# Layer 1's self-attention: score banks handed out and masked in pairs

## The chip, the cores and the metric

The kernel runs on one core of a Trainium2 chip. The metric is the device time of one execution in microseconds (us). A core has five engines that run their own instruction queues side by side: TensorE (matmuls, PE in the profile; its weight loads are PEld), VectorE (DVE), ScalarE (ACT), GpSimd (POOL) and SyncE (SP). Matmuls write into PSUM, which has eight banks of 512 fp32 columns on 128 partitions; VectorE and ScalarE carry the results into SBUF.

## The reference, cut to what matters

A two-layer decoder on 32 batches of 100 tokens of width 256: in each layer self-attention, cross-attention to a context, and a mixture of experts. The change is in layer 1's self-attention, which has 16 heads of width 16 and no softmax: scores above the diagonal are set to zero and multiplied with the values as they are.

```python
kqv = x @ W1 + b1                       # x is layer-normed, (32, 100, 256)
k, q, v = jnp.split(kqv, 3, axis=-1)    # each to (32, 16 heads, 100, 16)
mask = jnp.tril(jnp.ones((t, t), dtype=bool))
attn = jnp.where(mask, jnp.einsum('bhqd,bhkd->bhqk', q, k), 0.0)
out = jnp.einsum('bhqk,bhkd->bhqd', attn, v)
...
return out @ W2 + b2                    # added to x
```

## The kernel before, in words

The stages follow each other: layer 0's three parts, then `l1_attn`, `l1_xattn` and `l1_ffn`. All arithmetic is fp32. The activations lie in SBUF as 25 tiles of 128 rows (`self.x`), so a batch of 100 rows straddles tiles.

`l1_attn` begins with work of the next stage (`ahead`: 15 value projections of the cross-attention), turns the first seven tiles of norm rows (`turn`, `norm_turn`), projects queries and keys of the first four batches (`proj`) and then loops over the batches. Step b issues on TensorE, in this order:

- S, `scores(b)`: 16 small matmuls of 32 rows by 100 columns, heads in four row groups r = 0 to 3, that go round four banks, one per row group (400 of its 512 columns are used).
- P, `proj(b0 + 4, i)`: one of four projections for the next four batches. ScalarE copies the result out (one or two copies, L973, L976).
- V, `vals(b + 1)`: the values of the next batch; two VectorE adds carry them out (L986).
- Z, `values(b - 1)`: masked scores times values, of the batch before; ScalarE copies them out (L1022).
- O, `out(b - 2)`: output projection of a tile that is complete, in 25 of the steps; one VectorE add (L261).
- Turns: in the fourth step of a group of four batches, two of `norm_turn` for tiles of a later group; in a few steps one for the cross-attention (`next_norm`, `later`). A copy on VectorE or ScalarE in turn carries them out (L151, L150).

The masks are VectorE's: in `scores`, four multiplications with `keep`, the transposed lower triangle, each from one bank of PSUM into an `s` tile of SBUF (L1005). VectorE also adds the rows that GpSimd gathers from layer 0's experts (`gather0`, L1264 and L1269, two for each tile, spread over the first three steps of a group), and computes norm statistics and norm rows (L197 to L209). In the later groups nothing is left to gather.

The order on TensorE is the program's (`manual_schedule`). On the other engines a planner sets the order at compile time, by its own costs and by what is ready; each engine then runs its queue strictly in that order, with semaphores between the engines.

PSUM is handed out by tag: `self.psum.tile(..., bufs=n)` gives one of n buffers, and the taker waits until the previous user's last reader is done. Here all helpers (`bank_s`, `bank_m`, `bank_z`, `bank_t`) take from one tag of eight banks, in TensorE's order.

Of the kernel before, what the change touches and what calls it, by code (L numbers as in the profile page):

```python
# [9 lines left out]
F32 = mybir.dt.float32  # L10
# [3 lines left out]
ALU = mybir.AluOpType  # L14
AX = mybir.AxisListType

P = 128
NB = 32
T = 100
# [80 lines left out]
class Kernel:  # L100
# [26 lines left out]
        return self.tc.tile_pool(name=f"ps{name}", bufs=1, space=bass.MemoryType.PSUM)  # L127

    def bank(self, tag):
        if tag not in self.n_banks:  # L130
            tag = "t"
        return self.psum.tile([P, 512], F32, tag=tag, name=f"ps_{tag}", bufs=self.n_banks[tag])

    def bank_s(self):
        return self.bank("s")
# [91 lines left out]
    def norm_turn(self, f, n, xn, bank):  # L227
        pt = bank[:, : NK * n * P].rearrange("p (k c) -> p k c", k=NK)
        for k in range(NK):
            for j in range(n):  # L230
                self.nc.tensor.transpose(  # L231
                    pt[:, k, j * P : (j + 1) * P], xn[:, j, k * P : (k + 1) * P], self.ident,
                )
        self.evac(self.xnT[:, :, f * P : (f + n) * P], pt)
# [687 lines left out]
    def l1_attn(self):  # L922
        nc, tc, a = self.nc, self.tc, self.a
        with ExitStack() as st:
            self.psum = st.enter_context(self.banks("l1a", t=8))
            wk, wq, wv, wo, bqk, bv, bo, xbo = self.w1a
            cp = st.enter_context(tc.tile_pool(name="c1a", bufs=1))
            pool = st.enter_context(tc.tile_pool(name="p1a", bufs=2))
            for f in range(FRONT1[0]):
                self.gather0(pool, f)  # L930
            keep = self.tri(cp, "keepT", 1, -1, 1.0, 0.0)
# [18 lines left out]
            q, k, s, later = {}, {}, {}, deque()  # L950
# [39 lines left out]
            def rows_of(r):  # L990
                return slice(32 * r, 32 * r + 32)


            def scores(b):
                cols = slice((b % 4) * T, (b % 4 + 1) * T)
                ps = [self.bank_s()[:T, : 4 * T].rearrange("p (c j t) -> p c j t", c=2, j=2) for _ in range(4)]
                for c in range(2):
                    for j in range(2):
                        for r in range(4):
                            self.mm(ps[r][:, c, j, :], [(  # L1000
                                k[b // 4][rows_of(r), c, cols], q[b // 4][rows_of(r), c, j, cols]
                            )])
                for r in range(4):
                    t = s[b, r] = pool.tile([T, 2, 2, T], F32, tag="s", name="s", bufs=8)
                    nc.vector.tensor_tensor(  # L1005
                        t.rearrange("p c j t -> p (c j) t"), ps[r].rearrange("p c j t -> p (c j) t"),
                        self.mid(keep, 4), ALU.mult,
                    )

            def values(b):  # L1010
                pz = self.bank_z()[:, : 2 * T].rearrange("p (c t) -> p c t", c=2)
                for c in range(2):
                    for j in range(2):
                        for r in range(4):
                            nc.tensor.matmul(  # L1015
                                pz[rows_of(r), c, :], lhsT=vs[b % 3][:, 8 * c + 2 * r + j, :],
                                rhs=s[b, r][:, c, j, :], start=(j == 0), stop=(j == 1),
                            )
                for r in range(4):
                    del s[b, r]  # L1020
                for z, cols in self.z_parts(b):
                    nc.scalar.copy(z, pz[:, :, cols])  # L1022
# [33 lines left out]
            with tc.manual_schedule(engines={mybir.EngineType.PE}):  # L1056
# [17 lines left out]
                for b in range(NB + 2):  # L1074
                    i = b % 4
                    b0 = b - i
                    if b < NB:
                        scores(b)
                    if b0 + 4 < NB:
                        proj(b0 + 4, i)  # L1080
                    if b + 1 < NB:
                        vals(b + 1)
                    if 0 < b <= NB:
                        values(b - 1)
                    if b > 1:
                        out(b - 2)
                    if b0 + 8 < NB:
                        fs = group(b0 // 4 + 2)
                        if i < 3:
                            self.gather0(pool, fs[i], self.last_row)  # L1090
                            self.norm_stats(fs[i], FRONT1)
                        else:
                            turn(fs[0], 2)
                            turn(fs[2], 1)
                    if later:
                        later.popleft()()
                    if waiting:
                        next_norm()
# [996 lines left out]
```

## Time and profile before

| | |
|---|---|
| median of 3 runs | 2956.52 us (2954.38 to 2960.02) |
| the profiled execution | 2956.08 us, its span 2954.3 us |
| TensorE busy | 2851.3 us, 97% of the span |
| VectorE busy | 1787.6 us, 61% |
| ScalarE busy | 1412.4 us, 48% |
| `l1_attn`'s loop over batches | about 1620 to 1793 us of the span |

The profile is of one execution. A row of the timeline gives the start and length in us, the engine, the line, the operation with its tiles (out<-in) and form, and how many instructions it merges; in brackets how long the engine's queue stood idle before and what ended that. A matmul's row is one of TensorE, with the matching weight loads in a row of PEld; fp32 matmuls appear as two instructions each. `L156` is the helper `mm`, so the tiles tell its callers apart: `ps_t<-qT,kT` are scores, `ps_t<-xnT,wB` projections, `ps_t<-wB,xnT` values' inputs, `ps_t<-s,v` (L1015) values, `ps_t<-wB,zT` output projections. The end of a matmul is modelled, so a busy TensorE may in part be waiting: a stretch of the same work that is longer than usual, with an idle bracket at its weight loads, is a wait.

### The profile page before, as it was taken

The page shows a single profiled execution, that of the slowest core. Times are in us where ns is not written, and L with a number is a line of the kernel's source. Part 1 is how long each engine was busy: PE and PEld are TensorE (multiplying, and loading weights), DVE is VectorE, ACT ScalarE, POOL GpSimd, SP SyncE. Part 2 cuts the span into 40 slices and gives each one's busy share as a digit, 9 for nine tenths or more (in the row PEclk, how much of TensorE's full clock was granted, in tenths as well). Part 3 has the DMA queues.
Part 4 walks back from the last instruction along what each step waited for, and adds up shares of the span by engine and source line. Part 5 has one row for each costly group of instructions (what it writes and reads, how often), then busy time and mean ns, then how long its engine had stood idle before and what let it go on. Part 6 is the DMA issues. An engine that isn't in the chain of part 4 may idle for free. (4 is left out here: it accounts for less than half of the span.)

```text
span 2954.3 us, 66469 instructions
## 1 busy us (share of the span) xinstructions
PE 2851.3 (97%) x26012; PEld 2172.6 (74%) x26012; DVE 1787.6 (61%) x5120; ACT 1412.4 (48%) x4261; POOL 913.0 (31%) x1040
## 2 busy tenths in 40 slices
PE   8999999999999999999998999999999999999993
PEld 7777777677777766888886667777777777776672
DVE  6666665577777762222224878676676776776553
ACT  5555555467676641222223224565666565657320
POOL 3222221266666536100003621011302213123373
PEclk9999999999999989999999999999999999999996
DMA  9880000000000004564553100010000000000396
GB/s 319 269 290 1 1 1 1 12 15 16 16 16 16 10 29 147 191 223 181 194 215 112 49 4 10 6 38 25 26 10 13 10 9 16 12 11 5 97 227 189
DMA packets 127510, 224.11 MB, mean 76 GB/s; under 512 B 39470, under 2 KB 105446, under 8 KB 120401
## 3 DMA queue, kind: packets, MB, share of 16 engines
q1 hardware_dynamic: 97264, 125.64, 13.3%
q0 software_dynamic: 26640, 90.80, 9.3%
q8 instruction: 210, 3.44, 0.5%
q10 hardware_dynamic: 3280, 3.28, 0.3%
q14 instruction: 116, 0.94, 0.1%
HBM read 152.09 MB, written 112.56 MB: 90 GB/s over the span
## 5 line engine op out<-in xcount | busy, mean ns | idle before, releaser
L1691 POOL DMA_INDIRECT x_d<-xr,slot x200 | 195.4, 977 | 676.0 <-ACT eT L786 556.3
L156 PE MATMUL ps_t<-xnT,wA 128*128 128x200 f32 (+1 forms) x1608 | 330.9, 350 | 1.5 <-DMA wA<-in_wq 1.0
L156 PE MATMUL ps_t<-cT,q 128*128 128x361 f32 x832 | 317.3, 470 | 0.0
L786 ACT COPY eT<-ps_t 124x384 f32<-124x384 f32 (+1 forms) x416 | 193.6, 474 | 224.7 <-PE ps_t L785 224.5
L156 PEld LDWEIGHTS ps_t<-xnT,wA 128*128 128x128 f32 x1608 | 272.1, 191 | 32.4 <-issue 14.5
L776 ACT ACTIVATE wBx<-ps_t,m 128x361 f32<-128x361 f32 x416 | 235.8, 568 | 121.7 <-DVE m L773 117.7
L535 DVE TENSOR_REDUCE m<-ps_t 100x1 f32<-100x361 f32 x512 | 239.6, 524 | 48.3 <-PE ps_t L156 48.1
L156 PE MATMUL ps_t<-xT,w 128*128 128x256 f32 (+1 forms) x1276 | 260.2, 364 | 0.7 <-ACT xT L150 0.7
L773 DVE TENSOR_REDUCE m<-ps_t 128x1 f32<-128x361 f32 x416 | 218.3, 526 | 60.3 <-PE ps_t L156 58.3
L156 PEld LDWEIGHTS ps_t<-xT,w 128*128 128x128 f32 x1276 | 223.7, 190 | 36.2 <-issue 9.3
L785 PEld LDWEIGHTS ps_t<-ident,wBx 128*124 128x124 f32 x1248 | 156.1, 139 | 123.4 <-issue 68.2
L358 POOL TENSOR_TENSOR e<-e,rz 100x400 f32<-100x400 f32 x128 | 109.3, 854 | 406.3 <-DVE rz L357 396.8
L557 ACT ACTIVATE e<-ps_t 121x300 f32<-121x300 f32 x512 | 173.9, 426 | 119.0 <-PE ps_t L156 118.9
L785 PE MATMUL ps_t<-ident,wBx 128*124 128x128 f32 x1248 | 203.9, 275 | 5.3 <-DVE m L1627 2.1
L354 ACT ACTIVATE e<-s,m 100x100 f32<-100x100 f32 x512 | 186.1, 365 | 20.7 <-DVE m L348 20.0
L156 PE MATMUL ps_t<-wA,cT 128*124 128x512 f32 x384 | 195.5, 597 | 0.0
L778 DVE TENSOR_SCALAR wBx<-wBx,sums 128x361 f32<-128x361 f32 x416 | 172.9, 416 | 9.9
L1344 DVE TENSOR_TENSOR h<-ps_t,g 128x256 f32<-128x256 f32 (+1 forms) x145 | 58.2, 401 | 188.4 <-ACT g L1343 188.4
L156 PEld LDWEIGHTS ps_t<-q,k 32*121 32x121 f32 x3072 | 127.9, 181 | 36.0 <-issue 11.3
L797 PEld LDWEIGHTS ps_t<-eT,v 124*64 124x64 f32 x3072 | 133.1, 137 | 16.4 <-ACT wBx L776 5.6
L1343 ACT ACTIVATE g<-ps_t 128x256 f32<-128x256 f32 (+1 forms) x145 | 52.9, 365 | 190.9 <-PE ps_t L156 190.9
L1280 POOL DMA_INDIRECT w<-w_d,wid x29 | 29.5, 1017 | 371.0 <-PE ps_t L1371 337.4
(329 smaller groups left out, 5817.8 us busy)
## 6 DMA issues: line engine op xcount, KB each, us to landing
x_d<-fill SPq DMA_DIRECT2D x16, 1284.0 KB, 22.2
we<-in_wexp SPq DMA_DIRECT2D x32, 384.0 KB, 4.6
cT<-in_ctxT SPq DMA_DIRECT2D x64, 186.0 KB, 2.3
xe_d<-zero SPq DMA_DIRECT2D x8, 1024.0 KB, 16.3
xe<-x_d SPq DMA_DIRECT2D x24, 321.0 KB, 3.8
sum<-fill SPq DMA_DIRECT2D x10, 640.0 KB, 8.9
xe<-xe_d SPq DMA_DIRECT2D x24, 256.0 KB, 2.7
y_d<-y SPq DMA_DIRECT2D x24, 256.0 KB, 8.4
```

Of the source, the lines that this page charges most:

```text
L156: self.nc.tensor.matmul(out, lhsT=l, rhs=r, start=(i == 0), stop=(i == n - 1))
L354: nc.scalar.activation(t[:, i, :], s[:, i, :], AF.Exp, bias=m[:, i : i + 1], accum_out=rz[:, i : i + 1])
L358: nc.gpsimd.tensor_tensor(t[:, h, :], t[:, h, :], self.last(rz[:, h], T), ALU.mult)
L535: got = nc.vector.tensor_reduce(m[:, j, o : o + 1], ps[r], AX.X, ALU.max, negate=True)
L557: nc.scalar.activation(t[:, r], ps[r].rearrange("p (c t) -> p c t", c=NKC), AF.Exp)
L773: self.after = nc.vector.tensor_reduce(m, ps, AX.X, ALU.max, negate=True)
L776: nc.scalar.activation(t, ps, AF.Exp, bias=m, accum_out=z)
L778: nc.vector.tensor_scalar(t, t, z, None, ALU.mult)
L785: nc.tensor.transpose(pt[:, c, :], es[n % 5][:, c * KC : (c + 1) * KC], self.ident)
L786: self.after = nc.scalar.copy(eT[:, :, i * P : i * P + w], pt[:, :, :w])
L797: nc.tensor.matmul(pz[64 * j : 64 * j + 64, i, :], lhsT=v[:, c, h * 64 : (h + 1) * 64], rhs=eT[:, c, o : o + T], start=(c == 0), stop=(c = ...
L1691: got = nc.gpsimd.indirect_dma_start(out=self.x1_d[:, :], out_offset=bass.IndirectOffsetOnAxis(ap=slot[:, j, k : k + 1], axis=0), in_=xr[: ...
```

## The change

`l1_attn` no longer takes banks, but pairs of neighbouring banks from a tag of four buffers. Everything that asked for a bank gets the first bank of a pair and leaves the second empty. `scores` takes two pairs; row groups 0 and 1 write the two banks of the first, 2 and 3 those of the second. One VectorE instruction then masks both banks of a pair (800 columns per partition, the mask repeated eight times) into an `s` tile twice as large, of which there are half as many; `values` reads the same numbers from slices of it.

```diff
     def bank(self, tag):
+        if not self.n_banks:
+            return self.pair()[:, 0, :]
...
+    def pair(self):
+        return self.psum.tile([P, 2, 512], F32, tag="t", name="ps_t", bufs=4)
...
-            self.psum = st.enter_context(self.banks("l1a", t=8))
+            self.psum = st.enter_context(self.banks("l1a"))
...
-                ps = [self.bank_s()[:T, : 4 * T].rearrange("p (c j t) -> p c j t", c=2, j=2) for _ in range(4)]
+                ps = [self.pair()[:T, :, : 4 * T].rearrange("p r (g t) -> p r g t", g=4) for _ in range(2)]
                 for c in range(2):
                     for j in range(2):
                         for r in range(4):
-                            self.mm(ps[r][:, c, j, :], [(
+                            self.mm(ps[r // 2][:, r % 2, 2 * c + j, :], [(
                                 k[b // 4][rows_of(r), c, cols], q[b // 4][rows_of(r), c, j, cols]
                             )])
-                for r in range(4):
-                    t = s[b, r] = pool.tile([T, 2, 2, T], F32, tag="s", name="s", bufs=8)
+                for h in range(2):
+                    t = pool.tile([T, 2, 4, T], F32, tag="s", name="s", bufs=4)
                     nc.vector.tensor_tensor(
-                        t.rearrange("p c j t -> p (c j) t"), ps[r].rearrange("p c j t -> p (c j) t"),
-                        self.mid(keep, 4), ALU.mult,
+                        t, ps[h], keep.unsqueeze(1).unsqueeze(1).to_broadcast([T, 2, 4, T]), ALU.mult
                     )
+                    for r in range(2):
+                        s[b, 2 * h + r] = t[:, r].rearrange("p (c j) t -> p c j t", c=2)
```

## The prediction

> **What bounds the kernel now.** First the page: TensorE is busy nearly throughout, and the chain that ended last is mostly its matmuls.
>
> ```profile
> PE 2851.3 (97%) x26012; PEld 2172.6 (74%) x26012; DVE 1787.6 (61%) x5120; ACT 1412.4 (48%) x4261; POOL 913.0 (31%) x1040
> ```
>
> The stage that changes runs from 1620 to 1793 us of the span, 6% of it. I cut it at its groups of four batches (busy time by windows; columns: window, its length, then busy us and instructions of each engine, granted clock, DMA):
>
> ```profile
> 1665.08:1688.20 23.12, 22.95 (x315) 15.82 (x314) 20.58 (x57) 6.30 (x17) 17.34 (x18) 1.00 0.12 37
> 1734.62:1755.69 21.07, 21.07 (x311) 14.59 (x310) 15.06 (x39) 5.82 (x15) 3.96 (x6) 1.00 0.01 2
> ```
>
> A group that also gathers the next tiles' rows (first line) has VectorE busy 20.58 of 23.12 us and takes 2 us longer than one that doesn't. TensorE looks full in both, so the busy share hides the difference. The answer for the mask's line shows it:
>
> ```profile
> L1005 DVE TENSOR_TENSOR s<-ps_t,keepT x128: 531/564/576, 1624.4 to 1789.7; 100x400 f32<-100x400 f32 x128
>   PEld ps_t L156: 8.4, 30
>   PEld ps_t L1015: 2.4, 7
> ```
>
> TensorE's weight loads wait for masks, 30 times in scores. The timeline of batches 8 and 9 shows where:
>
> ```profile
> 1668.38 0.90 PE L1015 MATMUL ps_t<-s,v 100*32 100x100 f32 x32
> 1669.09 2.00 DVE L1005 TENSOR_TENSOR s<-ps_t,keepT 100x400 f32<-100x400 f32 x4
> 1669.20 1.13 PE L156 MATMUL ps_t<-wB,zT 128*128 128x256 f32 x4
> 1670.26 0.65 PEld L156 LDWEIGHTS ps_t<-qT,kT 32*100 32x100 f32 x6 [0.33 <-DVE s L1005]
> 1670.26 1.83 PE L156 MATMUL ps_t<-qT,kT 32*100 32x100 f32 x32
> 1671.14 0.78 PEld L156 LDWEIGHTS ps_t<-qT,kT 32*100 32x100 f32 x26 [0.24 <-DVE s L1005]
> ```
>
> The scores of batch 9 take 1.83 us where undisturbed ones take 0.96: their banks are still being masked for batch 8. Batch 8's scores ended at 1666.04, but VectorE was in norms and gather adds until 1669.09. Summing, over all scores, their start-to-next-start less 0.89 gives 11.3 us of such waiting, in batches 1, 2, 3, 5, 6, 9, 10, 13, 14, 17, 18 and a trace of it in 21. Elsewhere TensorE sets the pace.
>
> **The change, part by part.** *The masks.* 128 instructions of 400 columns become 64 of 800. One takes 0.564 us; four in a row start 0.48 apart (1669.086, 1669.571, 1670.052, 1670.533) and cover 2.00. For 400 columns the spacing is 0.481. The same kind of operation on 256 columns (L261) takes 0.42, so 144 more columns cost 0.14, about 1 ns each. An 800-column mask is thus 0.56 + 400 x 1.04 = 0.98 us long, and 0.48 + 0.42 = 0.90 apart. Saved per batch: 4 x 0.481 - 2 x 0.90 = 0.13 us of VectorE, 4 us in all. Bounds: 1.12 us long if the join saves nothing (2 x 0.56), 0.83 if only columns count. I take 0.98, on the slope between two rows. Where TensorE waits for nothing, the 4 us are worth nothing.
>
> The Trainium skill (Perfetto Trace Analysis, Optimizing Scalar/DVE Operations) says that a VectorE operation on PSUM carries some 125 ns of overhead and that larger operations raise throughput when that engine is saturated; by that figure the join would save 64 x 0.125 = 8 us of VectorE. The same section says that an engine that is not saturated but causes bubbles on others is better served by smaller instructions; that speaks against this change, and in the rows above VectorE is 89% busy in one group and 71% in the other.
>
> *The ring.* Before, eight banks are handed out in turn: four to scores, one each to projection (P), values' inputs (V), values (Z), output projection (O), and one for each turn of norm rows. So a bank comes round after eight takings, and next batch's scores take this batch's. After, `bank` takes a whole pair, and there are four. Per batch: S1, S2, P, V, Z, O. Z takes the pair of S1, O that of S2, the next S1 and S2 take those of P and V. The new waits on TensorE, with what is queued behind each:
> - Z(b-1) waits for the first mask of batch b. Behind it in TensorE's queue: O, turns, next scores; so everything.
> - O (or the turn) waits for the second mask; S1 for P's copies on ScalarE; S2 for V's two adds; P and V for Z's copies and O's add.
>
> The old wait of scores for the previous masks is gone, as these masks are done by then.
>
> How much slack has Z? From an undisturbed batch (starts 1659.24, 1660.14, 1661.58, 1662.54, 1663.36): S 0.90, P 1.44, V 0.96, Z 0.82; O to the next S is 1.06 (1743.61 to 1744.67). Z comes P + V = 2.40 us after P starts. The first mask needs 0.98, and 0.05 to be seen (1671.09 to 1671.14). So it may start 1.37 us after P's start for free, and each us beyond is on the path. Before, the next scores came 4.28 us after P's start (P, V, Z, O) and four masks with their signal need 3 x 0.481 + 0.56 + 0.05 = 2.06: a slack of 2.2 us. The pair costs 0.85 us of slack a batch.
>
> *One gathering group, worked out.* S(8) runs at 1665.08 as before and Z(7) is ready at 1668.38. Masks of 8 begin at 1669.09; the first is free at 1669.09 + 0.98 + 0.05 = 1670.12: Z(7) waits 1.74. O at 1670.94, the second mask free at 1669.09 + 0.90 + 1.03 = 1671.02: waits 0.08. S(9) at 1672.08 (V's adds end before), over at 1672.98, against 1672.02 in the trace: +0.96. Masks of 9 come in VectorE's queue at 1675.18, now 0.13 earlier, 1675.05; first one free at 1676.08, Z(8) ready at 1672.98 + 2.40 = 1675.38: waits 0.70. O at 1676.90, waits 0.08; S(10) at 1678.04, over at 1678.94 against 1678.11: +0.83. Masks of 10 were at 1679.24, behind O's add; that comes some 0.55 later, so they start near 1679.8, and are free at 1680.83, before Z(9) at 1681.34: no wait. S(11) has none either. So a group's 1.8 us of waits become 2.6: **+0.83**.
>
> *The sum.* Such groups are those of batches 4, 8, 12 and 16: 4 x 0.83 = 3.3. Batches 0 to 3: TensorE waits for the same late masks in either arrangement (4.6 us of the 11.3), and I put nothing. Batches 20 on gather no more, masks follow scores at once, and Z has its slack; only at 20, whose masks start at 1737.45 behind norm rows, 1.94 after P: 1.94 - 1.37 = 0.57, less the 0.15 that batch 21 waits now, +0.4. Batch 29 has neither P nor O, so S(30) takes the very pairs of S(29), at 1783.24; their masks start at 1781.75, and the second is free at 1781.75 + 0.90 + 1.03 = 1783.68: +0.4. Sum: 3.3 + 0.4 + 0.4, **+4 us**. With masks of 1.12 us each of the some ten waits is 0.14 longer, and the 0.13 a batch that pulled the later masks forward is gone, which adds 2 to 3 more: +8. With masks of 0.83 us the same terms turn round: +2.
>
> Costed at nothing: the same matmuls, as columns and row groups stay and the four row groups still write four banks; the second bank left empty in every other pair; the `s` tiles, half as many and twice as large, freed by the same Z; the 15 copies of the layer-1 values ahead of the stage (1592 to 1607), which ScalarE takes in 0.58 of every 0.86 us, so that four banks suffice; the hand-over to the next stage at 1793.7. If that cover fails, each costs one copy, 0.6 us. No DMA is added; the POOL gathers (1.01 us each) wait now and then for a mask (3.5 us in 6 waits) and move with it.
>
> The sum is made against the profiled execution, 2956.08 us (span 2954.3); the median shown is 2956.52, 0.44 above. 2956.5 + 4 = **2960.5**.
>
> **The rivals.** *Slower, order.* The order on VectorE is the planner's, from its own costs. With TensorE held in Z it may take more gather work (0.85 to 0.95 us an add) ahead of a mask. For: 1.7 us of such adds already stand ahead of batch 8's masks, and the group holds six. Against: TensorE's order is fixed, masks are early in it. It decides once a mask starts over 1.37 us late; two more adds a group put 1.8 x 4 = 7 on top: 2968, and all six up to 2978.
>
> *Faster, waits gone.* If masks stood right behind their scores, neither ring would bind, and the 11.3 us of waits go, in part: half of them is -6, 2950.5; all, 2945. For: VectorE is 11% idle even in the heavy groups, and gains 4 us. Against: the ring makes TensorE less free to run ahead.
>
> *No change.* VectorE alone sets the gathering groups: its work shrinks 0.13 a batch, and the ring's waits only replace the scores' waits: 2956 to 2957.
>
> **How the numbers follow.** The measurement tells apart about 0.2%, 5.9 us. My case has 0.55, own range 2958.5 to 2964.5; of it 0.24 lies above 2962.4, by the longer mask. The order rival has 0.28, faster 0.12, no change 0.05. So slower 0.24 + 0.28 = 0.52, same 0.31 + 0.05 = 0.36, faster 0.12. From 2952 to 2973 the range takes in my case and no change, and leaves out 0.08 of the order rival above and 0.10 of the faster one below.
>
> **What would show it.** Masks: 64 of 0.98 us. The scores' waits on L1005 nearly gone; L1015 waiting some 1.7 and 0.7 us per gathering group; windows of batches 20 to 27 the same as before, +0.1. It is wrong if the 8-to-12 window is shorter than 22.8, or if the masks' queue places differ by more than one gather add.

## The result, and the profile after

Before: 2955.14 us (median of 6 runs, 2952.4 to 2960.02). After: 2964.95 us (2962.38 to 2969.11). The ratio is 1.0034, 95% interval [1.0024, 1.0044]: slower by 9.8 us where 4 were forecast. The profiled execution of after took 2966.97 us (span 2965.2), 10.9 more than that of before.

The engines' line of the page of after, in the same columns as before:

```profile
PE 2844.9 (96%) x26012; PEld 2167.1 (73%) x26012; DVE 1785.2 (60%) x5056; ACT 1413.2 (48%) x4261; POOL 915.3 (31%) x1040
```

VectorE issues 64 instructions fewer, 2.4 us of work less. TensorE runs the same 26012 matmuls, with 6.4 us less of modelled busy time, as some of its waiting now stands between matmuls instead of inside a run of them.

The windows of after, cut at each group's first scores (window, its length, then busy us and instructions of PE, PEld, DVE, ACT, POOL, granted clock, DMA share, GB/s). The granted clock is the share of its full speed at which TensorE was let run:

```profile
1620.14:1645.73 25.59, 19.68 (x267) 13.06 (x266) 20.34 (x48) 5.10 (x13) 19.78 (x20) 0.93 0.27 78
1645.73:1669.08 23.35, 20.81 (x307) 14.21 (x306) 18.48 (x44) 5.66 (x15) 9.51 (x9) 1.00 0.13 36
1669.08:1693.45 24.37, 21.84 (x315) 15.06 (x314) 20.26 (x50) 6.42 (x17) 18.94 (x19) 1.00 0.12 35
1693.45:1718.10 24.65, 22.69 (x312) 15.63 (x311) 19.08 (x45) 6.14 (x17) 9.55 (x10) 0.93 0.08 23
1718.10:1743.76 25.66, 23.95 (x319) 16.65 (x318) 19.63 (x47) 6.99 (x18) 12.18 (x13) 0.93 0.01 2
```

Batches 16 to 19 of before, for comparison:

```profile
1710.99:1734.61 23.62, 23.48 (x319) 16.36 (x318) 19.88 (x55) 6.78 (x18) 12.08 (x13) 1.00 0.01 2
```

| group of batches | before, us | after, us | more | clock after |
|---|---|---|---|---|
| 0 to 3 | 22.02 | 25.59 | +3.57 | 0.93 |
| 4 to 7 | 22.09 | 23.35 | +1.26 | 1.00 |
| 8 to 11 | 23.12 | 24.37 | +1.25 | 1.00 |
| 12 to 15 | 22.79 | 24.65 | +1.86 | 0.93 |
| 16 to 19 | 23.62 | 25.66 | +2.04 | 0.93 |
| 20 to 23 | 21.08 | 21.53 | +0.45 | 1.00 |
| 24 to 27 | 20.54 | 20.54 | 0 | 1.00 |
| 28 to the stage's end | 17.44 | 17.73 | +0.29 | 1.00 |

The sum is +10.7; S(0) starts 0.83 earlier, so the stage ends 9.9 later, and 1.0 of the 10.9 lies behind it. The column to look at is the clock: in every one of these windows of before it is 1.00, and after it is 0.93 in three groups, those with the largest loss. Over the whole span the two lose nearly the same to half clock (49.2 us before, 48.1 after): after loses 5.1 more in this stage and 6.3 less outside it.

From the answer for the mask's line, after, with who waited for it (engine, tile, line: us, times):

```profile
L1010 DVE TENSOR_TENSOR s<-ps_t,keepT x64: 949/979/991, 1624.1 to 1799.1; 100x800 f32<-100x800 f32 x64
...
  PEld ps_t L1021: 17.2, 22
  PE ps_t L1021: 12.5, 9
  PEld ps_t L161: 4.7, 12
```

Before, the weight loads that waited for masks were those of scores (8.4 us in 30 waits); now they are those of Z (L1021, 17.2 us in 22). The timeline of after around batch 8 shows one such wait (TensorE's and VectorE's rows):

```profile
1671.43 1.03 PE L161 MATMUL ps_t<-wB,xnT 128*100 128x256 f32 x4
1671.47 1.70 DVE L1275 SCALAR_TENSOR_TENSOR x_sb<-yk,wA,x_sb 128x256 f32<-128x256 f32 x2
...
1673.09 1.88 DVE L1010 TENSOR_TENSOR s<-ps_t,keepT 100x800 f32<-100x800 f32 x2
1674.12 0.89 PE L1021 MATMUL ps_t<-s,v 100*32 100x100 f32 x32 [1.67 <-DVE s L1010]
1674.88 0.86 DVE L1275 SCALAR_TENSOR_TENSOR x_sb<-yk,wA,x_sb 128x256 f32<-128x256 f32 x2
1675.02 1.13 PE L161 MATMUL ps_t<-wB,zT 128*128 128x256 f32 x4
1675.67 0.47 DVE L991 TENSOR_TENSOR v<-ps_t,wB 100x128 f32<-100x128 f32 x2
```

V's last matmul would let Z(7) start at 1672.39 (0.96 after V's start); two gather adds hold the masks until 1673.09, the first mask is done at 1674.07, and Z starts at 1674.12: 1.73 us late. O follows 0.90 after Z instead of 0.82. Then two gather adds stand before V's adds, where before had one.

**What the table's clock is.** TensorE's granted clock drops to 0.50 three times in the stage of after, each time for 3.413 us, from 1638.96, 1700.40 and 1724.30. The distances, 61.440 and 23.893 us, are 18.0 and 7.0 times that length, so the clock is decided on a fixed grid. Windows laid on this grid (same columns):

```profile
1635.59:1639.00 3.41, 1.57 (x64) 1.45 (x64) 2.71 (x6) 1.74 (x5) 2.64 (x4) 0.99 0.13 38
1639.00:1642.41 3.41, 3.41 (x17) 1.85 (x10) 1.89 (x2) 0.07 (x1) 2.77 (x3) 0.50 0.40 115
1649.24:1652.65 3.41, 1.87 (x36) 1.35 (x36) 3.41 (x7) 0.74 (x3) 1.43 (x2) 1.00 0.00 0
1673.13:1676.54 3.41, 2.42 (x49) 1.81 (x53) 3.41 (x9) 0.39 (x2) 3.10 (x2) 1.00 0.15 46
1697.03:1700.44 3.41, 1.58 (x35) 1.31 (x36) 3.41 (x8) 0.69 (x3) 2.95 (x5) 0.99 0.00 0
1700.44:1703.85 3.41, 3.41 (x40) 2.61 (x39) 3.18 (x14) 0.20 (x1) 2.80 (x3) 0.50 0.37 105
1720.92:1724.33 3.41, 1.70 (x36) 1.05 (x35) 3.41 (x7) 1.18 (x4) 0.22 (x1) 1.00 0.02 5
```

Read the PE column of the windows at full clock: 1.57, 1.58 and 1.70 busy of 3.41 (46 to 50%), and the next window runs at half; 1.87 and 2.42 (55 and 71%), and it does not. Those two hold the Z waits of batches 4 and 8, as long as the one of batch 16, but cut by the grid: their first part lies in the window ahead. So a wait of 1.7 us costs itself, and with bad luck in the grid also up to 1.7 us (half of 3.41) behind it. In before the least busy window of this stage was 77% busy, as its waits of 0.9 us lay inside scores, apart from each other:

```profile
1632.60:1636.00 3.40, 2.63 (x40) 1.59 (x38) 3.30 (x10) 0.29 (x2) 3.22 (x5) 1.00 0.16 46
```

A modelled end counts a wait inside a run of matmuls as busy, and that flatters before. An estimate that gives each matmul the time it takes undisturbed (32 of scores 0.89 us, 32 of values 0.82, four of a projection 1.44, four of V or O 0.96, a transpose 0.125) fills the three windows of after ahead of half clock to 47, 41 and 45%, the two others to 51 and 62%, and no window of before to less than 64%. The Trainium skill (TensorE: Matmul & The Clock Gate, Part 1) describes such a free-running window of 3413 ns and a half clock after an idle one; here half a window of waiting was enough.

### The profile page after: what moved, and what is told of

It reads as the page before. It is cut to its first block, busy times and chain, and to the rows that moved or that the text cites. A ratio compares the mean times of both kernels' runs of the same rounds, so it can differ in the third digit from the quotient of the medians.

```text
span 2965.2 us, 66418 instructions
## 1 busy us (share of the span) xinstructions
PE 2844.9 (96%) x26012; PEld 2167.1 (73%) x26012; DVE 1785.2 (60%) x5056; ACT 1413.2 (48%) x4261; POOL 915.3 (31%) x1040
```

## The experiments

They ran on other chips than the pair above, on which before itself takes 2986 to 2992 us; so only ratios to before on the same chip are compared. The changed kernel itself was set against before on the first pair's chip alone; its one run elsewhere is in 7 and 8.

**1 and 2. Which half of the change: the pairs for all, or the joined mask?** The first keeps the joined masks, with pairs for scores alone and four single banks for the rest:

```diff
-        if not self.n_banks:
-            return self.pair()[:, 0, :]
...
-        return self.psum.tile([P, 2, 512], F32, tag="t", name="ps_t", bufs=4)
+        return self.psum.tile([P, 2, 512], F32, tag="p", name="ps_p", bufs=2)
...
-            self.psum = st.enter_context(self.banks("l1a"))
+            self.psum = st.enter_context(self.banks("l1a", t=4))
```

> The joined masks stay, but only scores take pairs (a ring of two pairs of their own); all other takers share four single banks, so no bank lies empty. Theory 'ring' (the loss comes from eight places becoming four, so that values and the output projection wait for this batch's masks): the waits at values go, scores again wait only for the batch before, VectorE keeps its 4 us; 2952 to 2956, that is 9 to 13 us under the changed kernel. Theory 'join' (an 800-column mask releases its first bank later than two short ones): still slow, 2962 to 2966. Theory 'order' (the planner's new order on VectorE, with gather adds ahead of masks): the planner leaves the order of the changed kernel, so still slow by about half, 2960.

Measured: 0.9984 [0.9975, 0.9993]. The second keeps the pairs for all, with one mask per bank:

```diff
-                    nc.vector.tensor_tensor(
-                        t, ps[h], keep.unsqueeze(1).unsqueeze(1).to_broadcast([T, 2, 4, T]), ALU.mult
-                    )
                     for r in range(2):
+                        nc.vector.tensor_tensor(t[:, r], ps[h][:, r], self.mid(keep, 4), ALU.mult)
```

> Pairs for everyone as in the changed kernel, but a mask for each bank (four of 400 columns a batch), so the join is undone and the ring of four places kept. Theory 'ring': as slow as the changed kernel or slower, since VectorE loses the 4 us again; 2964 to 2969. Theory 'join': back to 2955 to 2957. Theory 'order': the planner's order on VectorE here is that of the kernel before in nearly every group, so half of the loss goes: 2960.

Measured: 1.0039 [1.0026, 1.0053]. The joined mask with another ring is not slower than before; the ring of pairs without the joined mask is. The mask's line in the first (score tiles are now `ps_p`, from L159; values L1019):

```profile
L1008 DVE TENSOR_TENSOR s<-ps_p,keepT x64: 948/980/992, 1626.4 to 1800.0; 100x800 f32<-100x800 f32 x64
...
  PEld ps_p L159: 10.4, 19
  PE ps_p L159: 6.0, 12
...
  PEld ps_t L1019: 0.5, 2
```

The masks last the same 980 ns, and the waits are back in scores; Z hardly waits (0.5 us). Theory 'order' falls with it: from the first mask to the last, VectorE's queue in this kernel has the order of the changed kernel, operation by operation, and the loss is gone all the same.

**3. The split alone, masks not joined.** Before, with four banks for scores and four for the rest:

```diff
-            self.psum = st.enter_context(self.banks("l1a", t=8))
+            self.psum = st.enter_context(self.banks("l1a", s=4, t=4))
```

> The kernel before with its eight banks split: four for scores, four for the others; four masks a batch. With the first run it tells what the join alone is worth in one and the same ring. Theory 'ring': scores wait for the masks of the batch before, as they do now; 2954 to 2957. The join is then worth this time less the first run's, by the spacing of masks 1 to 3 us. Theory 'join': this one is under the first run's time by 6 us or more.

Measured: 0.9996 [0.9987, 1.0005]. Its VectorE queue is that of before. Between this one and the second, the ring differs, with the size of the `s` tiles and few places in VectorE's queue (one gather add goes ahead of the masks of batch 16): 0.43%, 12.8 us (2983.55 to 2996.30). Between it and the first, the join, with the planner's order: 0.12%, 2.6 us, in the direction of the 4 us of VectorE work saved, but with intervals that overlap. The windows of the second kernel, at batches 8 and 12, show how much of the 12.8 is clock:

```profile
1676.10:1703.90 27.80, 23.83 (x317) 16.47 (x316) 21.06 (x58) 6.45 (x17) 17.53 (x19) 0.94 0.10 30
1703.90:1730.10 26.20, 23.58 (x315) 16.20 (x314) 19.66 (x53) 6.12 (x16) 9.52 (x10) 0.93 0.08 21
```

It has half-clock stretches in each of its first five groups, together worth 11.9 us at full rate; the third kernel has 5.1. So some 6.8 of the 12.8 us go with the clock in these two profiles. By the mean clock recorded for every run (0.9788 over the second's five, 0.9828 over the third's eleven) it is about 12 us over the whole execution (an estimate: 0.0040 of 2990), as much as the two differ. That the ring costs time is shown; how its price divides into waits and the half clock behind them is not.

**4 to 6. Masks first.** If the loss is the masks' lateness against the ring's slack, it goes when masks come early. An order edge puts a step's gather adds, and the norm rows of a turn, behind the step's masks:

```diff
-                self.norm_turn(f, n, self.norm_rows(f, n, bias=bo), self.bank_m())
+                self.norm_turn(f, n, self.norm_rows(f, n, bias=bo, after=self.masked), self.bank_m())
...
-                    nc.vector.tensor_tensor(
+                    self.masked = nc.vector.tensor_tensor(
...
-                            self.gather0(pool, fs[i], self.last_row)
+                            self.gather0(pool, fs[i], self.masked)
```

In the changed kernel:

> The changed kernel with its four pairs, but gather adds and norm rows of a step are put behind the masks of that step in VectorE's queue (an order edge on the same engine; no other work changes). The ring has 1.37 us of slack per batch for a late mask. Theory 'ring', by lateness: masks begin within 0.2 us of their scores, so the waits at values (1.7, 0.9 us a group and up) go; about 8 to 11 us under the changed kernel, 2954 to 2957, unless turns now wait for their norm rows, which would give back 1 us a group. Theory 'join': no change in what a mask costs, 2962 to 2965.

In the kernel before:

> The kernel before (eight single banks, four masks a batch) with the same order edges as the last run: gather adds and norm rows of a step behind its masks. Theory 'lateness' (what both kernels wait for is a late mask, the ring only sets how late is free): the 11 us of waits in scores go for the most part, 6 to 10 us under the kernel before, ratio 0.9965 to 0.998; and the four pairs then cost little, so that this run and the last one differ by under 4 us. Rival 'pairs are worse by themselves': this run is under the last one by 8 us or more, ratio 0.9945 or less.

In the first experiment's kernel:

> Both cures together: scores alone take pairs, the others four single banks, joined masks, and the order edges. Theory 'lateness': with masks early neither ring binds, so it stands within 3 us of the two runs with the order edges alone, ratio 0.996 to 0.998; VectorE's 4 us are worth 0 to 3. Theory 'ring alone': the two gains add up, 0.16 and 0.3 per cent, ratio 0.995 to 0.9955.

Measured: 0.9970 [0.9959, 0.9980], 0.9956 [0.9940, 0.9973] and 0.9963 [0.9949, 0.9977]. By ratios to before, each from its own chip, the same edges take 0.64% off the changed kernel (1.0034 without them, measured above), 0.44% off before and 0.21% off the first kernel. The first two gained more than was expected: 19 us where 8 to 11 were, and 0.9956 where 0.9965 to 0.998 were. With early masks the three PSUM layouts lie within 0.14% of each other, about 4 us, with overlapping intervals: the ring costs hardly anything when nothing is late, and the gains do not add up. From the answer for the mask's line in the changed kernel with early masks:

```profile
L1010 DVE TENSOR_TENSOR s<-ps_t,keepT x64: 950/981/993, 1622.8 to 1792.2; 100x800 f32<-100x800 f32 x64
...
  PEld ps_t L1021: 7.0, 17
  PEld ps_t L161: 1.8, 8
  PE ps_t L1021: 1.4, 3
```

Z's weight loads wait 7.0 us instead of 17.2. Before with early masks, 2972.84 us against 2986.28 on its chip, has the lowest ratio of all versions, with an interval that overlaps those of the other two, and beats both kernels. Its price is new waits of 1.35 to 1.5 us at two turns, whose norm rows now come late.

**7 and 8. The pair once more**, one profiled run of each, on the chip of the fifth and sixth:

> The kernel before once more, for a profile on the chip of these runs: waits in scores of 11 us by the ring of eight, in the same batches as in the first profile. If GpSimd's bias adds hold a VectorE operation somewhere (an operation of VectorE that lasts 1.6 us or more over its median while GpSimd adds), the first or second group is 2 to 4 us longer than in the first profile.

> The changed kernel once more, for a profile on the same chip: 3.0 us of waits in each of the groups of batches 4 and 8, 3.4 to 3.8 in the next two, at values and behind. If the 1.79 us operation of the first group (norm statistics' L207, beside GpSimd's bias adds) belongs to the kernel, it is there again in the same place; if it is an accident of timing, it is elsewhere or absent, and the first group is then 3 us shorter than 25.6.

Measured: 2983.54 and 2987.32 us. Here both have 6.8 us of half clock in the stage (3.4 lost), and after is 3.8 us slower, close to the forecast's 4, but only 1.0 above the median of before's eight runs on this chip (2986.28). From the first group to the sixth, after is longer by -0.1, +1.2, -0.9, +2.6, +0.9 and +0.5 us. The first group is 26.40 us before and 26.34 after: each kernel has a gather add of 2.88 us there beside GpSimd's adds, and L207 is not held again. So the accident moved, and the group did not become shorter, against the expectation. One pair of runs decides little: before also has a stall of 2.95 us in the values of batch 9, in which TensorE's matmuls come a few at a time, its brackets say "issue" (it waited for nothing that the profile shows), and VectorE and ScalarE stand too. The first pair has no such bracket in the stage.

**9 to 11. Without GpSimd's bias adds.** In the first groups GpSimd adds a bias row to the tiles of a turn (L229 after, L224 before) while VectorE does gather adds; two of these take 1.70 us at 1671.47 above, beside GpSimd's adds, and 0.87 without them. These kernels leave the adds out (the norm rows without `bias=bo`), in the changed kernel, in before and in the first experiment's kernel:

```diff
-                self.norm_turn(f, n, self.norm_rows(f, n, bias=bo), self.bank_m())
+                self.norm_turn(f, n, self.norm_rows(f, n), self.bank_m())
```

> The changed kernel without the adds on GpSimd that put the output projection's bias on the rows of x in this stage (that part of the computation is left out). The planner's order on VectorE stays. It tells how much of the loss is GpSimd holding VectorE. Theory 'ring': waits at values in every gathering group stay, 2 to 3 us each, since the gather adds ahead of the masks stay (each at 0.48 us instead of up to 0.95); this run is 4 to 7 us over its twin without the change. Theory 'GpSimd' (the loss is the accident that a VectorE operation is held in the first group and TensorE's clock falls): the two twins agree within 2 us.

> The kernel before without the same adds on GpSimd (left out likewise). With no add to share the way to SBUF with, the masks come 1 to 2 us sooner in each gathering group: waits in scores fall from 11 us to 3 to 6, the time by 5 to 10 us under the kernel before, ratio 0.9965 to 0.9985. The stage has no VectorE operation over 1.5 us and TensorE's clock stays at 1.00.

> Pairs for scores alone, four single banks for the others, joined masks (the first run), without the same adds on GpSimd (left out likewise). Theory 'ring': 1 to 4 us under the kernel before without the adds, by what the join saves VectorE; 5 to 10 under the changed one without them. Theory 'join': as slow as the changed one without the adds.

Measured: 1.0000 [0.9986, 1.0014], 1.0005 [0.9995, 1.0015], 0.9996 [0.9987, 1.0006]. Theory 'ring' missed: its 4 to 7 us between the twins are not there, and the first kernel is 2.7 us under the changed one, not 5 to 10. The twins agree within 2 us (2986.04 and 2987.04), as theory 'GpSimd' had it, and before gained nothing. That the pairs lose nothing here would fit the lateness: with gather adds of 0.48 us ahead of them masks come earlier, and Z waits 0.51 and 0.93 us in each of the groups of batches 4 and 8. But then before should have gained, and why it didn't is open: its profile has 10.2 us lost at half clock in the first three groups, behind stalls like the one above. Its "issue" brackets on TensorE sum to 6.7 us in the stage, those of the changed kernel to 1.2. So the ring's price was there with GpSimd's adds and is not seen without them.

**12. TensorE kept busy in the waits.** If the half clock is part of the loss, work in the gaps should save it. Behind V's two adds in `vals`:

```diff
+FILL = {3: 3, 5: 2, 6: 1, 9: 2, 10: 1, 13: 2, 17: 2}
...
-                pm = self.bank_m()[:T, :D]
+                two = self.pair()
+                pm = two[:T, 0, :D]
...
+                for _ in range(FILL.get(b, 0)):
+                    self.mm(two[:T, 1, :D], [(self.xn_of(i, b), wv[:, i, :]) for i in range(NK)])
```

> The changed kernel with TensorE kept at work where it waits for a mask: behind the values' inputs of batches 3, 5, 6, 9, 10, 13 and 17 the same matmuls are repeated (3, 2, 1, 2, 1, 2, 2 times, 0.96 us each) into the empty second bank of their pair, which nobody reads. VectorE's queue keeps its masks and adds for the values in their places; the last gather adds of a group move by a place or two. Theory (the ring's waits cost 4 us, and the gaps that they leave halve TensorE's clock, which costs the rest): the repeats stand in the waits of 1.7 to 2.0 and 0.9 us before Z and cost under 1 us, half-clock stretches in the stage fall from three to one at most, and the ratio to before is 1.0010 to 1.0025, against the changed kernel's 1.0034. Rival (the clock has no part, the loss is waits alone): nothing is gained, the repeats cost what they overhang, 0 to 2 us, ratio 1.0034 to 1.0042, with or without half-clock stretches.

Measured: 1.0083 [1.0066, 1.01], outside both. The kernel did not do what I meant. The timeline at batch 8 (V is L163, values L1026, V's adds L994; TensorE's and VectorE's rows):

```profile
1688.49 1.88 DVE L1015 TENSOR_TENSOR s<-ps_t,keepT 100x800 f32<-100x800 f32 x2
1690.29 0.87 DVE L1280 SCALAR_TENSOR_TENSOR x_sb<-yk,wA,x_sb 128x256 f32<-128x256 f32 x2
1691.07 0.48 DVE L994 TENSOR_TENSOR v<-ps_t,wB 100x128 f32<-100x128 f32 x2
1691.61 3.74 PE L163 MATMUL ps_t<-wB,xnT 128*100 128x256 f32 x8 [3.75 <-DVE v L994]
1695.27 1.56 PE L1026 MATMUL ps_t<-s,v 100*32 100x100 f32 x32
```

The repeats write the same pair as V, so they were made to wait for V's adds, which stand behind the masks and two gather adds: they lengthened the wait to 3.75 us and then stood between it and Z. The question as put is not answered. But the accident doubles the suspected cost: all four gathering groups now have a gap of 3.7 to 4.1 us, and each is followed by half clock, for two windows in the first two groups and one in the others. The windows around the gap at batch 4:

```profile
1655.80:1659.25 3.45, 0.61 (x3) 0.17 (x1) 3.45 (x6) 1.11 (x2) 1.47 (x3) 1.00 0.00 0
1659.25:1666.10 6.85, 5.94 (x42) 4.05 (x43) 3.44 (x14) 0.21 (x1) 5.59 (x5) 0.50 0.27 76
```

The eight repeated matmuls took 3.74 us at half clock; four of the same kind take 1.03 at full clock.

## Why the prediction was right or wrong

The direction, the whole range (2952 to 2973) and the waits forecast for the gathering groups held; the size was 6 us short. The case's own range, 2958.5 to 2964.5 (+2 to +8), was missed: 2964.95 and +9.8. The whole range reached further up to take in the rival "order", which is not what came, so that the result lies inside is in part luck. Step by step, on the profiled executions of the first pair (+10.9):

- *The masks*: 64 of 979 ns, 0.90 or less apart, against 0.98 and 0.90. Right. By the Trainium skill's 125 ns an operation (Perfetto Trace Analysis, Optimizing Scalar/DVE Operations) the estimate was 0.25 us a batch; the spacing shows some 0.06 per pair, 0.12 a batch.
- *The ring*: Z waits for the first mask, O for the second, scores no longer for masks. Right: 1.73 and 0.08 at batch 8, against 1.74 and 0.08. The first three experiments show the ring to be the cause, and not the join or the order on VectorE; experiments 4 to 6 show that it charges for lateness, and in 9 to 11, without GpSimd's adds, no price of it was seen.
- *One gathering group*, +0.83 forecast, +1.26 and +1.25 measured in groups 4 to 7 and 8 to 11, where the clock stays at 1.00. The failing term is Z(8)'s wait of 0.70: it is 0.93, and S(9) waits 0.21 for V's adds, because the planner put two gather adds ahead of them instead of one. The planner moved one add there, not the two or six of the rival "order". Over four groups it makes +1.7.
- *"Costed at nothing: the same matmuls."* This step failed in the first pair. They are the same in number and form, but three stretches run at half clock. In the groups of batches 12 and 16 that adds 0.61 and 0.79 over the undisturbed gathering groups, less than 1.7 each, since a late TensorE finds the next masks done. I had read the clock column of before as 1.00 and taken it to stay. What changed with the ring is that waits come as one of 1.7 us instead of two of 0.9 in scores. That this brings the half clock is argued from the grid's windows; in the second pair before loses as much to it as after, there behind an operation for norm rows (L209) that ran 2.05 us beside GpSimd's adds.
- *Batches 0 to 3: nothing.* This failed in the first pair too, +3.57 less the 0.83 of the earlier start. Step 0 has no Z and no O, so S(1) takes the pairs of S(0) and waits for both masks (1.72, 0.89), and Z of step 2 waits 3.07 for a mask behind a norm operation of VectorE that ran 1.78 us (below). Then the half clock: the projection behind it took 3.04 us instead of 1.61. This projection alone is 1.4 us of the loss. In the second pair the first groups are equal, so this term is not shown to belong to the change.
- *Batch 20* +0.4, measured +0.45; *S(30)* +0.4, measured +0.29 in the last group; batches 24 to 27 equal, as forecast.

So: 4.1 forecast, 1.7 from the second waits, 1.4 from the clock in two groups, 2.7 from the first group (half of it clock), and 1.0 behind the stage, which I did not trace: 10.9. Of the rivals, "waits gone" did not come by itself; masks right behind their scores, its condition, are what the order edges of the fifth experiment made.

## What to carry to other kernels

When buffers are handed out in a ring, count who takes which place after whom: half the places means that another, nearer instruction waits, and the latest producer decides its price; putting that producer first in its queue was worth more here (0.44%) than either layout. Price a wait of TensorE not by its length alone: look at the granted clock behind it. In the first pair two of the four gathering groups had half clock behind one wait of 1.7 to 2.0 us, and none behind two of 0.9. Before trusting a filler or a shared buffer, look in the timeline at what it waits for.

## What the runs showed of the hardware

**The clock's grid.** In all profiles of this case half-clock stretches of the stage last whole multiples of 3.413 us and start on a grid of that length, and what counts is how busy TensorE was in the grid's window ahead. By modelled matmul times, every full-clock window of these stages that was under 42% busy was followed by half clock, and none over 77%; between, both occur. By the estimate above, with undisturbed times, the border is sharper: of 682 full-clock windows in 14 profiles all 23 under 41.5% were followed by half clock, none over 47.5%, and 7 of the 14 between.

**A VectorE operation held until GpSimd is done.** The timeline of after in the first group (some rows):

```profile
1633.84 2.09 POOL L229 TENSOR_TENSOR x_sb<-x_sb,wB 128x256 f32<-128x256 f32 x3
1634.17 1.78 DVE L207 TENSOR_SCALAR rstd<-mv 128x3 f32<-128x3 f32 x1
1636.32 1.86 DVE L1010 TENSOR_TENSOR s<-ps_t,keepT 100x800 f32<-100x800 f32 x2
1637.43 0.89 PE L1021 MATMUL ps_t<-s,v 100*32 100x100 f32 x32 [3.01 <-DVE s L1010]
1639.27 3.04 PE L161 MATMUL ps_t<-xnT,wB 128*128 128x400 f32 x4
```

An operation on 3 columns, 0.17 us elsewhere, ends with GpSimd's third add; the masks stand behind it in VectorE's queue, Z behind them, and the last line is the projection at half clock. In the changed kernel with early masks two gather adds beside five GpSimd adds took 4.13 us. Elsewhere the two engines only slow each other (two gather adds 1.70 instead of 0.87). The Trainium skill (SBUF — State Buffer, SBUF: two separate sides) speaks of an exclusive lock for the whole of one instruction; here a VectorE operation was held over several of GpSimd's adds. Of the 11 profiles with these adds ten have one or two such operations in the stage (1.78 to 3.61 us), each ending 0.04 to 0.3 us after the last of two to five adds; the first profile of before has none, nor have the three kernels without these adds.
